# Folding the attention weights two banks a tick, and the first layer norm ahead of the folded weights

## The chip, the cores and the metric

One core of a Trainium2 chip runs the whole program. The metric is the device time of one execution, in microseconds (us). Engines are named as in the profile: PE is TensorE (matmuls), PEld its weight loads, DVE is VectorE, ACT is ScalarE, POOL is GpSimd, and SP is the engine whose queue issues nearly all DMAs here.

## What is computed

The input x has 4 images of 384 channels and 32 x 32 pixels, all in float32. Layer 0 adds a four-way selective scan of the group-normalised image, followed by a layer norm and a GELU. Layer 1 takes the pixels as tokens and adds causal attention and then a mixture of four expert networks, of which each token uses two. Cut to what matters:

```
x = x + gelu(layernorm(selective_scan_4_directions(groupnorm(x))))
t = tokens(x)                                  # 4 x 1024 x 384
n = layernorm(t)
q, k, v = n @ Wq, n @ Wk, n @ Wv
t = t + softmax(causal(q @ k.T * 384**-0.5)) @ v
t = t + top2_of_4_experts(layernorm(t))        # 384 -> 1536 -> 384 each
```

Since q k^T = n (Wq Wk^T) n^T, the kernel needs only the product of the two weights. And since the layer norm subtracts a mean that is linear in the token, the subtraction can be put into the weights: with the centring matrix C = I - 1/384, it uses C Wq Wk^T C and C Wv, and the tokens then only have to be scaled. Making these two 384 x 384 matrices is called folding here; it is done once.

## The kernel before

P = 128 partitions, M = 3 blocks of channels, B = 4 images, L = 1024 pixels.

**Ticks.** The program is written out by hand in ticks, by the loop at the end of `hybrid_kernel`. One tick handles one unit of the scan: 32 channels times 4 states of one image and direction, on 128 partitions and 1024 pixels. There are 4 x 192 units (`IMAGE` = 192). In each tick DVE multiplies (v, L561) and scans (h, L567), ACT makes the decay of two ticks ahead (da, L554), and POOL multiplies the scan of the tick before (L584). Every fourth tick PE sums four h into y with 16 matmul passes (L609). There are seven h buffers and three da buffers.

**What goes beside the scan.** Everything else is a Python generator that issues some instructions and then yields: "wait" with a number of ticks, "pe" with an estimate of PE time that is taken off a budget, or "inner", which puts the next piece into the following tick ahead of its scan. In a tick come, in this order: the decay, what was deferred to this tick, v and the product, inner pieces, the scan, y, the fetches for later ticks (`fetch`), one step of the image preparation (`preparation`, group norm and projections of an image to come), then the list `side` in its order, and last `waiting[0]`, which works off `behind(b)`: the attention and the experts of image b. Its budget per tick is `PACE_E` = 3.3 us of estimated PE time and, during the attention, `PACE_A` = 4.4.

**One image after another.** When the last unit of image b has been summed, `evict` starts `finish(b)`, layer 0's layer norm and GELU (side list), and appends `behind(b)`, which waits until `finish(b)` has put b into `finished`. By the code this takes from tick 195 to tick 206 for image 0 and from 387 to 398 for image 1. `behind(0)` is through in tick 397. After tick 768 there are no more scans, and what is left of image 3 runs alone.

**Shared buffers.** Four PSUM banks (two until tick 192) and eight SBUF slots are shared by all generators; `take` waits for a tick in which one is free, `give` returns it. Both lists are first in, first out. `project_dt` (L408 onwards) of the preparation needs four slots at once and two banks at a time; `layernorm`, as `finish` uses it, needs two banks for `mu` (L652), three slots for squares (L672), and a bank for `var` (L679); its remaining steps are a subtraction on DVE (L660), a square root on ACT (L687), a reciprocal (L692), the spread `rb` (L698) and a product (L708). `finish` then adds x (L893).

**The fold.** In tick 192 `second()` opens new pools: `a0` with one buffer and `ht` with two, of 12 KB a partition each. `fold` is started. It loads the three weights, makes the two centring blocks on DVE (L728), and then takes one bank a job: six `pwt` jobs (18 matmul passes each, L746), which turn and centre one third of Wq or Wk; three `pg` jobs (6 passes, L757) for the product; three `pwv` jobs (6 passes, L769) for the centred Wv. Each job waits a tick, is copied out by ACT (L751, L762, L774), and only then is the next begun. `g_d` and `wv_d` in HBM receive the result (L765, L777), and `folded` is set; by the code, in tick 208. `w_extra` in `a0` holds Wv and the centring blocks.

**The first attention.** `attention(b)` waits for `folded`, takes four slots and loads the folded weights (L962, L964), scales the tokens in `scaled_tokens` (squares L905, `var_at` L914, `rs_at` L923, L925, L927 and L929, `rb_at` L934, and `axn` L948), and goes on to `pq` (L980), `pv` (L991) and the scores (L1009).

Of the kernel before, what the change touches and what calls it, by code (L numbers as in the profile page):

```python
# [8 lines left out]
F32 = mybir.dt.float32  # L9
AF = mybir.ActivationFunctionType  # L10
ALU = mybir.AluOpType
# [4 lines left out]
P = 128  # L16
B = 4
C = 384
M = C // P
HW = 32  # L20
L = HW * HW
# [28 lines left out]
def hybrid_kernel(  # L50
# [22 lines left out]
    nc = tc.nc  # L73
# [44 lines left out]
    class Shared:  # L118
# [20 lines left out]
        def give(self, *names):  # L139
# [33 lines left out]
    g_d = dram.tile([P, M, C], F32, tag="g", name="g_d")  # L173
    wv_d = dram.tile([P, M, C], F32, tag="wv", name="wv_d")
# [75 lines left out]
    scale = float(C) ** -0.5  # L250
# [463 lines left out]
    folded = []  # L714

    def fold():

        extra = pools["a0"].tile([P, M, L], F32, tag="a0", name="w_extra")
        extra = extra.rearrange("p m l -> p (m l)")
        vs = extra[:, : 2 * M * C].rearrange("p (j c d) -> p j c d", j=2, c=M)
        centre = extra[:, 2 * M * C : 2 * M * C + 2 * P].rearrange("p (j d) -> p j d", j=2)
        nc.sync.dma_start(vs[:, 0], wv.rearrange("(c p) d -> p c d", p=P))
        for same in range(2):
            nc.vector.scalar_tensor_tensor(  # L728
                centre[:, same, :], ident, float(same), mean_w, ALU.mult, ALU.subtract
            )  # L730
        def square(name):
            t = pools["ht"].tile([P, M, L], F32, tag="ht", name=name)
            t = t.rearrange("p m l -> p (m l)")[:, : 2 * M * C]
            return t.rearrange("p (j c d) -> p j c d", j=2, c=M)

        raw = square("w_raw")
        for j, w in enumerate((wq, wk)):
            nc.sync.dma_start(raw[:, j], w.rearrange("(c p) d -> p c d", p=P))
        wt = square("w_t")
        yield "wait", 2  # L740
        for j in range(2):
            for d in range(M):
                ps = yield from banks.take(f"pwt_{j}_{d}")
                for c in range(M):
                    for o in range(M):
                        nc.tensor.matmul(  # L746
                            ps[:, c * P : (c + 1) * P], raw[:, j, o, d * P : (d + 1) * P],
                            centre[:, int(o == c), :], start=(o == 0), stop=(o == M - 1),
                        )
                yield "wait", 1  # L750
                nc.scalar.copy(wt[:, j, d, :], ps[:, :C])  # L751
                banks.give(f"pwt_{j}_{d}")
        g = square("g_s")[:, 0]
        for m in range(M):
            ps = yield from banks.take(f"pg_{m}")
            for d in range(M):
                nc.tensor.matmul(  # L757
                    ps[:, :C], wt[:, 0, d, m * P : (m + 1) * P], wt[:, 1, d, :],
                    start=(d == 0), stop=(d == M - 1),
                )  # L760
            yield "wait", 1
            nc.scalar.activation(g[:, m, :], ps[:, :C], AF.Copy, scale=-scale)  # L762
            banks.give(f"pg_{m}")
        yield "wait", 1
        nc.sync.dma_start(g_d, g)  # L765
        for m in range(M):
            ps = yield from banks.take(f"pwv_{m}")
            for c in range(M):
                nc.tensor.matmul(  # L769
                    ps[:, :C], centre[:, int(c == m), :], vs[:, 0, c, :],  # L770
                    start=(c == 0), stop=(c == M - 1),
                )
            yield "wait", 1
            nc.scalar.copy(vs[:, 1, m, :], ps[:, :C])  # L774
            banks.give(f"pwv_{m}")
        yield "wait", 1
        nc.sync.dma_start(wv_d, vs[:, 1])  # L777
        folded.append(1)


# [119 lines left out]
    def scaled_tokens(b, yb):  # L900

        sqs = []
        for c in range(M):
            sq = yield from slots.take(f"sq_at_{b}_{c}", P, L)
            nc.scalar.activation(sq, yb[:, c, :], AF.Square)  # L905
            sqs.append(sq)

        var = yield from banks.take(f"var_at_{b}")
        for o, src in ((NH * P, [yb[:, c, :] for c in range(M)]), (0, sqs)):
            for h in range(NH):  # L910
                for c in range(M):
                    for q in range(4):
                        k = h * 512 + q * P
                        nc.tensor.matmul(  # L914
                            var[32 * q : 32 * (q + 1), o + h * P : o + (h + 1) * P],
                            mean_w[:, :32], src[c][:, k : k + P],
                            start=(c == 0), stop=(c == M - 1), tile_position=(0, 32 * q),
                        )
                yield "pe", 1.0
        slots.give(*[f"sq_at_{b}_{c}" for c in range(M)])  # L920
        rs = one.tile([P, NH, P], F32, tag=f"rs{NH}", name=f"rs_at_{b}")
        flat = rs.rearrange("p h t -> p (h t)")
        nc.scalar.activation(flat, var[:, NH * P : 2 * NH * P], AF.Square)  # L923
        yield "inner", 0
        nc.vector.tensor_tensor(flat, var[:, : NH * P], flat, ALU.subtract)  # L925
        banks.give(f"var_at_{b}")
        nc.scalar.activation(rs, rs, AF.Sqrt, bias=eps)  # L927
        yield "wait", 1
        nc.vector.reciprocal(rs, rs)  # L929
        backs = []  # L930
        for h in range(NH):
            rb = yield from banks.take(f"rb_at_{b}_{h}")
            for q in range(4):
                nc.tensor.matmul(  # L934
                    rb[:, q * P : (q + 1) * P],
                    ident[:, 32 * q : 32 * q + 1].to_broadcast([P, P]), rs[:, h, :],
                    start=True, stop=True,
                )
            backs.append(rb)
            yield "pe", 1.0  # L940
        while b > 0 and b - 1 not in stored:

            yield "wait", 1
        xn = pools["a0"].tile([P, M, L], F32, tag="a0", name=f"axn_{b}")
        yield "inner", 0
        for h in range(NH):
            s = bass.ts(h, 512)
            nc.vector.tensor_tensor(  # L948
                xn[:, :, s], yb[:, :, s], backs[h].unsqueeze(1).to_broadcast([P, M, 512]), ALU.mult
            )  # L950
            banks.give(f"rb_at_{b}_{h}")
        return xn

    def attention(b, yb, fx0):

        alone = b == B - 1
        while not folded:
            yield "wait", 1
        gw_ = []
        for name, w in ((f"wg_{b}", g_d), (f"wv_{b}", wv_d)):  # L960
            ta = yield from slots.take(f"{name}a", P, 2, C)
# [1 line left out]
            tb = yield from slots.take(f"{name}b", P, C)  # L963
            nc.sync.dma_start(tb, w[:, 2, :])  # L964
            gw_.append((ta[:, 0, :], ta[:, 1, :], tb))
        xn = yield from scaled_tokens(b, yb)
        qt = pools["ht"].tile([P, M, L], F32, tag="ht", name=f"qt_{b}")
        vt = pools["ht"].tile([P, L // P, C], F32, tag="ht", name=f"vt_{b}")

# [4 lines left out]
        for h in range(NH):  # L974
            for m in range(M):
                s = bass.ts(h, 512)
                name = f"pq_{b}_{m}_{h}"
                ps = yield from banks.take(name)
                for c in range(M):
                    nc.tensor.matmul(  # L980
                        ps, gw_[0][c][:, m * P : (m + 1) * P], xn[:, c, s],
                        start=(c == 0), stop=(c == M - 1),
# [4 lines left out]
        for i in range(L // P):  # L987
            name = f"pv_{b}_{i}"
            ps = yield from banks.take(name)
            for c in range(M):  # L990
                nc.tensor.matmul(  # L991
                    ps[:, :C], xn[:, c, i * P : (i + 1) * P], gw_[1][c],
                    start=(c == 0), stop=(c == M - 1),
# [411 lines left out]
    while t < NU + 4 or waiting or side or due or inner or parked:  # L1405
# [5 lines left out]
        if t == IMAGE:  # L1411
            second()
            side.append(fold())
# [77 lines left out]
```

## Time and profile before

| | us |
|---|---|
| three executions | 3745.99, 3749.89, 3752.34 |
| median | 3749.89 |
| the profiled execution, own time | 3747.14 |
| its span in the profile | 3745.0 |
| span until the end of image 0's scans (tick 192) | 675.3 |
| first matmul `pq` of attention 0, 1, 2, 3 | 767.3, 1580.6, 2392.6, 3143.9 |
| TensorE and VectorE busy in the last 663 us | 641.0, 87.9 |

The span runs from the first to the last instruction of the profile; 2.1 us of the execution lie outside it. All times in the text that follows are microseconds from the start of the span. A line of a timeline gives start, duration, engine, source line, operation, output and inputs with buffer numbers left out, and the count of instructions merged in it; brackets give the idle time of the engine before it and who ended it. Matmuls in float32 appear as two passes each, so a job of nine matmuls shows as 18.

### The profile page before, as it was taken

The page shows a single profiled execution, that of the slowest core. Times are in us where ns is not written, and L with a number is a line of the kernel's source. Part 1 is how long each engine was busy: PE and PEld are TensorE (multiplying, and loading weights), DVE is VectorE, ACT ScalarE, POOL GpSimd, SP SyncE. Part 2 cuts the span into 40 slices and gives each one's busy share as a digit, 9 for nine tenths or more (in the row PEclk, how much of TensorE's full clock was granted, in tenths as well). Part 3 has the DMA queues.
Part 4 walks back from the last instruction along what each step waited for, and adds up shares of the span by engine and source line. Part 5 has one row for each costly group of instructions (what it writes and reads, how often), then busy time and mean ns, then how long its engine had stood idle before and what let it go on. Part 6 is the DMA issues. An engine that isn't in the chain of part 4 may idle for free. (4 is left out here: it accounts for less than half of the span.)

```text
span 3745.0 us, 35189 instructions
## 1 busy us (share of the span) xinstructions
PE 3350.6 (89%) x11891; PEld 1529.0 (41%) x11891; DVE 2961.6 (79%) x2084; ACT 2085.8 (56%) x2832; POOL 1817.8 (49%) x776
## 2 busy tenths in 40 slices
PE   4666667789999999898999999889999998999999
PEld 1333333345333343344333344454344444544444
DVE  5999899988998998989998999999999982210000
ACT  4788888556666555566655555455554552412121
POOL 2777777555565565545555665455665650000000
PEclk7677777899999999999999999899999999999999
DMA  6665666645665756436666665455657551322321
GB/s 204 219 233 199 208 218 221 215 145 199 235 222 201 260 206 230 155 138 228 217 221 229 201 210 192 146 182 188 223 192 240 179 182 38 92 82 83 96 82 53
DMA packets 408019, 680.03 MB, mean 182 GB/s; under 512 B 33520, under 2 KB 279968, under 8 KB 407840
## 3 DMA queue, kind: packets, MB, share of 16 engines
q1 hardware_dynamic: 401632, 677.40, 53.0%
q8 instruction: 94, 1.54, 0.2%
q10 hardware_dynamic: 6208, 0.39, 0.1%
q14 instruction: 85, 0.70, 0.1%
HBM read 605.16 MB, written 72.55 MB: 181 GB/s over the span
## 5 line engine op out<-in xcount | busy, mean ns | idle before, releaser
L584 POOL TENSOR_TENSOR h<-h,bc 128x1024 f32<-128x1024 f32 x768 | 1816.7, 2370 | 1264.9 <-DVE v L561 1058.3
L567 DVE TENSOR_TENSOR_SCAN h<-da,v 128x1024 f32<-128x1024 f32 x768 | 1748.4, 2283 | 48.4 <-PE v L872 17.3
L554 ACT ACTIVATE da<-dt,a 128x1024 f32<-128x1024 f32 x768 | 886.5, 1162 | 868.1 <-DVE h L567 759.3
L1297 PE MATMUL fy<-ht,w 128*128 128x512 f32 x2304 | 1019.8, 599 | 7.5 <-ACT ht L1261 5.9
L1272 PE MATMUL ph<-fx,w 128*128 128x512 f32 x2304 | 1019.1, 598 | 3.8 <-DMA w<-in_w 2.9
L561 DVE TENSOR_TENSOR v<-du,bc 128x1024 f32<-128x1024 f32 x664 | 842.8, 1269 | 61.9 <-DMA du<-dts 25.9
L1297 PEld LDWEIGHTS fy<-ht,w 128*128 128x128 f32 x2304 | 435.6, 191 | 580.3 <-issue 551.0
L1272 PEld LDWEIGHTS ph<-fx,w 128*128 128x128 f32 x2304 | 433.4, 191 | 579.6 <-issue 529.5
L609 PE MATMUL y<-h,sel 128*32 128x512 f32 x3072 | 493.3, 657 | 91.2 <-POOL h L584 89.2
L1257 ACT ACTIVATE ht<-ph,b1s 128x512 f32<-128x512 f32 x384 | 257.9, 679 | 471.0 <-PE ph L1272 469.2
L1306 DVE SCALAR_TENSOR_TENSOR fy<-fy,b2s,tw 128x512 f32<-128x512 f32 x96 | 72.0, 750 | 423.0 <-PE fy L1297 423.0
L609 PEld LDWEIGHTS y<-h,sel 128*32 128x32 f32 x3072 | 96.6, 115 | 399.3 <-issue 220.3
L850 ACT ACTIVATE st<-turn,bt 128x128 f32<-128x128 f32 x832 | 244.2, 554 | 0.0
L872 PE MATMUL v<-ident,st 128*128 128x128 f32 x832 | 147.5, 337 | 86.2 <-DVE h L567 85.4
L1261 ACT ACTIVATE ht<-ht 128x3072 f32<-128x3072 f32 x64 | 176.9, 2764 | 0.8
L872 PEld LDWEIGHTS v<-ident,st 128*128 128x128 f32 x832 | 121.7, 175 | 127.7 <-DVE h L567 74.2
L554 ACT ACT_TABLE_LOAD x99 | 127.0, 1283 | 18.7 <-DMA dt<-dts 12.3
L425 PE MATMUL pdt<-xd,wdt 12*128 12x512 f32 x184 | 88.0, 813 | 45.7 <-ACT dt L433 22.6
L1079 PE MATMUL po<-pt,vt 128*128 128x256 f32 x480 | 102.8, 364 | 7.1 <-ACT pt L971 7.1
L1009 PE MATMUL ss<-axn,qt 128*128 128x512 f32 (+3 forms) x288 | 102.3, 503 | 3.9 <-ACT yb L1096 3.9
L1079 PEld LDWEIGHTS po<-pt,vt 128*128 128x128 f32 x480 | 90.4, 192 | 22.3 <-ACT pt L971 10.1
L1009 PEld LDWEIGHTS ss<-axn,qt 128*128 128x128 f32 x288 | 51.5, 196 | 47.1 <-issue 33.5
(208 smaller groups left out, 1612.3 us busy)
## 6 DMA issues: line engine op xcount, KB each, us to landing
bc<-rows SPq DMA_DIRECT2D x384, 512.0 KB, 4.7
w<-in_w SPq DMA_DIRECT2D x384, 384.0 KB, 6.0
dt<-dts SPq DMA_DIRECT2D x192, 512.0 KB, 4.5
du<-dts SPq DMA_DIRECT2D x192, 512.0 KB, 6.6
dts<-dt SPq DMA_DIRECT2D x48, 512.0 KB, 4.7
dts<-du SPq DMA_DIRECT2D x48, 512.0 KB, 5.3
fx<-t2d SPq DMA_DIRECT2D x12, 768.0 KB, 5.5
tw<-mkd SPq DMA_DIRECT2D x32, 256.0 KB, 6.2
```

The lines of the kernel that those rows point to most:

```text
L554: u["decay"] = nc.scalar.activation(u["da"], spread["dt4", n], AF.Exp, scale=a4[:, g, u["q"] : u["q"] + 1])
L561: return nc.vector.tensor_tensor(u["v"], spread["du4", n], spread["bc", n][:, 0, :], ALU.mult)
L567: nc.vector.tensor_tensor_scan(u["h"][:, ::step], u["da"][:, ::step], u["v"][:, ::step], 0.0, op0=ALU.mult, op1=ALU.add,)
L584: product = units[n]["product"] = nc.gpsimd.tensor_tensor(h, h, spread["bc", n][:, 1, :], ALU.mult)
L609: units[n]["row"] = nc.tensor.matmul(y, sel, h, start=first, stop=last, tile_position=(0, jj * DJ))
L850: nc.scalar.activation(st[:, 4 * h + t, :].rearrange("p (d i) -> p i d", i=NI)[:, i, :], ps[h][:, t * P : (t + 1) * P], AF.Copy, scale=bt[ ...
L872: nc.tensor.transpose(u["v"][:, t * P : (t + 1) * P], st[:, t, u["j"] * P : (u["j"] + 1) * P], ident)
L1079: nc.tensor.matmul(pv[:, o:], vt[:, j, m * P : (m + 1) * P], pts[step][j // 4][:, j % 4, o:], start=(alone and j == 0), stop=(j == nj - 1),)
L1257: nc.scalar.activation(ht[:, f, :], ps, AF.Identity, bias=bias)
L1261: nc.scalar.activation(ht, ht, AF.Gelu)
L1272: nc.tensor.matmul(ps, tiles[n][:, c, (f % 2) * P : (f % 2 + 1) * P], xns[h][:, c, :], start=(c == 0), stop=(c == M - 1),)
L1297: nc.tensor.matmul(pss[m], tiles[n][:, f, :], hts[fh][:, f, :], start=(fh == 0 and f == 0), stop=(fh == 1 and f == FH - 1),)
```

## The change

`fold` no longer uses `a0`. Wv and the centring blocks go into three of the shared slots (`va`, `vb`, `centre`), Wq and Wk are loaded first, and the result is collected in one `ht` tile, `both`. The jobs are functions that issue their matmuls into a bank and return the copy that is to follow. `by_twos` takes two banks at once, issues two jobs, and makes the two copies in the next tick, in which it also begins the next two jobs. The product and the centring of Wv form one list of six jobs. The slots are given back before the stores. `attention(0)` makes `scaled_tokens` first, then waits for `folded`, and then loads the folded weights; the attentions of the other images keep their order, without the wait.

```diff
-        extra = pools["a0"].tile([P, M, L], F32, tag="a0", name="w_extra")
...
         raw = square("w_raw")
         for j, w in enumerate((wq, wk)):
             nc.sync.dma_start(raw[:, j], w.rearrange("(c p) d -> p c d", p=P))
+        va = yield from slots.take("va", P, 2, C)
+        vb = yield from slots.take("vb", P, C)
+        centre = yield from slots.take("centre", P, 2, P)
+        wvs = wv.rearrange("(c p) d -> p c d", p=P)
+        nc.sync.dma_start(va, wvs[:, :2, :])
+        nc.sync.dma_start(vb, wvs[:, 2, :])
...
+        def by_twos(what, jobs):
+            for n in range(0, len(jobs), 2):
+                some = jobs[n : n + 2]
+                while not banks.ready(len(some)):
+                    yield "wait", 1
+                names = [f"{what}_{n + i}" for i in range(len(some))]
+                moves = [f(banks.now(name)) for f, name in zip(some, names)]
+                yield "wait", 1
+                for move in moves:
+                    move()
+                banks.give(*names)
+
+        yield "wait", 2
+        pairs = [(j, d) for d in range(M) for j in range(2)]
+        yield from by_twos("pwt", [lambda ps, j=j, d=d: turned_weight(j, d, ps) for j, d in pairs])
+        both = square("g_s")
+        jobs = [lambda ps, m=m: product(m, ps) for m in range(M)]
+        yield from by_twos("pg", jobs + [lambda ps, m=m: centred(m, ps) for m in range(M)])
+        slots.give("va", "vb", "centre")
+        nc.sync.dma_start(g_d, both[:, 0])
+        nc.sync.dma_start(wv_d, both[:, 1])
+        yield "wait", 1
         folded.append(1)
...
     def attention(b, yb, fx0):
 
         alone = b == B - 1
-        while not folded:
-            yield "wait", 1
+        if b == 0:
+            xn = yield from scaled_tokens(b, yb)
+            while not folded:
+                yield "wait", 1
         gw_ = []
         for name, w in ((f"wg_{b}", g_d), (f"wv_{b}", wv_d)):
             ta = yield from slots.take(f"{name}a", P, 2, C)
...
-        xn = yield from scaled_tokens(b, yb)
+        if b > 0:
+            xn = yield from scaled_tokens(b, yb)
```

`turned_weight`, `product` and `centred` issue the same matmuls as before into the bank they are given, and return the same ScalarE copies.

More of the change, by code (lines that the diff above doesn't have):

```diff
@@ L716, in fold @@
     def fold():
-        extra = pools["a0"].tile([P, M, L], F32, tag="a0", name="w_extra")
[L723 to L730, printed above, removed]
         def square(name):
@@ L738, in fold, with turned_weight, product @@
             nc.sync.dma_start(raw[:, j], w.rearrange("(c p) d -> p c d", p=P))
-        wt = square("w_t")
[L740 to L749, printed above, removed]
-                yield "wait", 1
[L751 to L755, printed above, removed]
+        va = yield from slots.take("va", P, 2, C)
[4 more added lines that the diff above has]
+        nc.sync.dma_start(vb, wvs[:, 2, :])
+        vs = (va[:, 0, :], va[:, 1, :], vb)
+        for same in range(2):
+            nc.vector.scalar_tensor_tensor(
+                centre[:, same, :], ident, float(same), mean_w, ALU.mult, ALU.subtract
+            )
+        wt = square("w_t")
+        def turned_weight(j, d, ps):
+            for c in range(M):
+                for o in range(M):
+                    nc.tensor.matmul(
+                        ps[:, c * P : (c + 1) * P], raw[:, j, o, d * P : (d + 1) * P],
+                        centre[:, int(o == c), :], start=(o == 0), stop=(o == M - 1),
+                    )
+            return lambda: nc.scalar.copy(wt[:, j, d, :], ps[:, :C])
+        def product(m, ps):
             for d in range(M):
@@ L760, in fold, with centred @@
                 )
[L761 to L767, printed above, removed]
+            return lambda: nc.scalar.activation(both[:, 0, m, :], ps[:, :C], AF.Copy, scale=-scale)
+        def centred(m, ps):
             for c in range(M):
                 nc.tensor.matmul(
-                    ps[:, :C], centre[:, int(c == m), :], vs[:, 0, c, :],
+                    ps[:, :C], centre[:, int(c == m), :], vs[c],
                     start=(c == 0), stop=(c == M - 1),
                 )
-            yield "wait", 1
-            nc.scalar.copy(vs[:, 1, m, :], ps[:, :C])
-            banks.give(f"pwv_{m}")
+            return lambda: nc.scalar.copy(both[:, 1, m, :], ps[:, :C])
+        def by_twos(what, jobs):
[18 more added lines that the diff above has]
+        nc.sync.dma_start(wv_d, both[:, 1])
         yield "wait", 1
-        nc.sync.dma_start(wv_d, vs[:, 1])
         folded.append(1)
@@ L956, in attention @@
         alone = b == B - 1
-        while not folded:
-            yield "wait", 1
+        if b == 0:
+            xn = yield from scaled_tokens(b, yb)
+            while not folded:
+                yield "wait", 1
         gw_ = []
```

## The prediction, made before the changed kernel ran

> **What bounds the kernel now.** I read the page's first part, then busy time by stage around the changed code, then who waited for whom on VectorE there, and last the timelines of each engine between 670 and 790 us.
>
> ```profile
> PE 3350.6 (89%) x11891; PEld 1529.0 (41%) x11891; DVE 2961.6 (79%) x2084; ACT 2085.8 (56%) x2832; POOL 1817.8 (49%) x776
> ```
>
> TensorE and VectorE are both full, but at different times, so the shares of the span decide nothing. The stage table (us; busy time of each engine, granted clock, DMA share) cuts where the changed code stands:
>
> ```profile
> core 0: us, PE busy (x) PEld busy (x) DVE busy (x) ACT busy (x) POOL busy (x), PEclk, DMA share, GB/s
> 675.30:765.50 90.20, 65.41 (x409) 37.76 (x409) 84.60 (x54) 53.25 (x60) 45.60 (x20) 0.78 0.53 190
> 765.50:1520.00 754.50, 727.50 (x2440) 317.18 (x2440) 705.23 (x504) 464.75 (x499) 423.00 (x180) 0.99 0.61 211
> 1520.00:1580.60 60.60, 43.84 (x276) 19.64 (x274) 59.82 (x42) 32.53 (x33) 28.82 (x13) 0.86 0.52 184
> ```
>
> From 675 to 765 us, where the weights are folded and the first attention waits, VectorE is busy 84.6 of 90.2 us and sets the pace; TensorE idles 25 us at a clock of 0.78. From 765 to 1520 us the first image's attention and experts hold TensorE for 727.5 of 754.5 us. From 1520 to 1580 us that work has run out: TensorE idles 17 of 60.6 us, VectorE is full. So work of image 0 that starts earlier finds a valley both in front of it and behind it.
>
> ```profile
> DVE rs_l L692 <- ACT rs_l L687: 1.8, 1, 1.8
> DVE rs_at L925 <- ACT rs_at L923: 1.6, 1, 1.6
> DVE axn L948 <- PE rb_at L934: 1.0, 1, 1.0
> ```
>
> These are all the named waits of VectorE from 676 to 772 us: 4.4 us in three places (columns: us in total, times, longest). That is the most which any reordering there can win on the engine that bounds.
>
> The ticks: each tick holds one scan of VectorE (L567). The two centre operations of `fold` come right behind the scan of tick 192, so scans can be numbered from there.
>
> ```profile
> 677.50 0.52 DVE L728 SCALAR_TENSOR_TENSOR w_extra<-ident,mean_w 128x128 f32<-128x128 f32 x2
> ...
> 740.41 1.43 DVE L893 TENSOR_TENSOR yb<-xr,yb 128x1024 f32<-128x1024 f32 x1
> ...
> 765.48 3.46 DVE L948 TENSOR_TENSOR axn<-yb,rb_at 128x1536 f32<-128x1536 f32 x2 [1.02 <-PE rb_at L934]
> ```
>
> Counted so, the last addition of `finish(0)` (740.41) stands ahead of scan 206, and `axn` (765.48) ahead of scan 211. `finished` is thus set in tick 206, and attention 0 held back until `folded`, in tick 208. TensorE and the DMA queue say the same:
>
> ```profile
> 711.43 4.21 PE L746 MATMUL pwt<-w_extra,w_raw 128*128 128x128 f32 x18
> 715.57 1.10 PE L679 MATMUL var_l<-sq_l,mean_w 128*32 128x128 f32 x24
> ...
> 739.38 0.64 PE L914 MATMUL var_at<-yb,mean_w 128*32 128x128 f32 x16
> ...
> 751.15 0.66 PE L914 MATMUL var_at<-sq_at,mean_w 128*32 128x128 f32 x8 [8.17 <-ACT sq_at L905]
> ...
> 767.29 1.98 PE L980 MATMUL pq<-axn,wg_0a 128*128 128x512 f32 x4
> ```
>
> ```profile
> 747.23 0.54 SPq L777 DMA_DIRECT2D wv_d<-w_extra  x1
> 747.82 0.42 SPq L962 DMA_DIRECT2D wg_0a<-g_d  x1
> ...
> 752.44 0.32 SPq L962 DMA_DIRECT2D wv_0a<-wv_d  x1
> 752.81 0.44 SPq L964 DMA_DIRECT2D wv_0b<-wv_d  x1
> 753.34 22.78 SPq L533 DMA_DIRECT2D bc<-rows  x4
> ```
>
> The loads of the folded weights issue at 747.8 to 753 us, 15 us before the first `pq` needs them: hidden today.
>
> **What the skill says.** *PSUM — Partial Sum Buffer*, "PSUM: the matmul accumulator": 8 banks of 2 KiB a partition. Here y and v take two each, so four are shared; two a tick is half of them. No run here shows the size itself. *ScalarE: Activation LUTs*, "What ACT_TABLE_LOAD costs": about 1283 ns, plus a drain of about 1380 ns. The trace has 1283 ns as the mean of 99, but no drain (a load from 716.17 for 1.28 us, the square root at 717.47), so I take 1.28 us. *TensorE: Matmul & The Clock Gate*, "What's actually happening": the clock halves after an idle window of some 3.4 us and comes back after as much steady work. The trace agrees in kind: granted clock 0.78 in the thin stage, 0.99 in the full one, and a `pwt` job of 18 matmuls at 2.17 to 2.3 us, once 4.21. *Perfetto Trace Analysis*, "Per-engine timelines" (DMA, HWDGE): the window shown for a queue's DMA leaves out the moving of data. The trace agrees: `wg_0a` shows 0.42 us on the queue and 5.6 us to landing.
>
> **The change, part by part.**
>
> *1. The fold itself.* Same matmuls (6 `pwt`, 3 `pg`, 3 `pwv` jobs), same 12 copies, same two centre operations. By the code: pairs of `pwt` in ticks 194, 195, 196; `pg` 0 and 1 in 197; `pg` 2 with `pwv` 0 in 198; `pwv` 1 and 2 in 199; stores in 200; `folded` in 201 instead of 208. Banks suffice: with two held by the fold, `finish(0)` still gets `mu` in 195 and 196 and `var` in 198.
>
> *2. Its crowd on TensorE.* In ticks 194 to 199 TensorE now has 6 x 2.3 (`pwt`) + 6 x 2.1 (`pg`, `pwv`) + 2 x 2.7 (`mu`) + 2.2 (one row) + 2 x 0.9 (`var`) = 36 us. From 681.3 us, in order and at that speed, the first half of `mu` ends at 693, the second at 700.5, the second `var` at 717.2; before it ended at 716.7. The second half of the subtraction L660 would start at 700.1 and waits 0.4 us. The reciprocal L692 starts at about 718.2 against 717.97, although a multiplication of 1.43 us (L441) has left its front (part 3). VectorE so loses 0.2 + 1.43 = +1.7 us. Bounds: 0, if the matmuls run as the fastest do; +12, if the clock is low (rival B).
>
> *3. Three slots for va, vb and centre.* From 192 to 200 three of eight slots are gone. `finish(0)` takes three more in 198, so two are left, and `project_dt` of image 1 (last m, second pair), which wants four in tick 198, starts in 201. All it issues moves along: one ScalarE copy (1.97 us), four softplus pieces with their table loads, four `pdt` matmuls, two multiplications of VectorE (1.43 and 1.37), four stores on SP's queue. Its results are first needed near tick 347: nothing waits. SP's stores then stand behind the `xr` loads of tick 204, which helps those. The square root of L687 no longer follows a softplus; I count one more table load, 1.28 us on ScalarE, covered by its lead of two ticks (it is busy 53 of 90 us). The moved multiplications cost VectorE the same later. Uncovered it would be +1.3.
> `preparation(1)` also ends three ticks later, so all of `preparation(2)` to about tick 348 shifts by three; due from 379 on.
>
> *4. The layer norm beside the fold.* `folded` no longer gates; `finished` in 206 does. But in 206 the budget is still at the slower pace, 3.3, not 4.4: the four steps of 1.0 use it up, and the rest of `scaled_tokens` goes on in 207. The subtraction L925 falls in 208 (before: 209), `axn` in 210 (before: 211). So two ticks of waiting win one. ScalarE's squares and square now have a tick between them and L925: its wait of 1.64 us goes. What is late next is `rb_at` at `axn`, 1.0 us, as before.
>
> *5. Weights after the layer norm.* The four loads (1.15 MB) are now issued in tick 210, behind the `bc` loads of tick 209. SP is held there by the product of tick 208, in today's trace until 753.3 us. Shifted by the 0 to 2 us of the parts above, `wg` issues at about 754.5 and lands 5.6 us later, at 760 to 761, as its measured time says; half of `axn` would be done at about 762. Cost between 0 (landed in time) and +4 us (if the `bc` megabyte in front delays it by its own landing time, 4.7, less what slack there is). I take +1. Behind a waiting `pq` stand the row matmuls of y, which free h buffers (seven), two ticks of cover. Pools: `axn` no longer waits for `w_extra` to be stored, nothing today.
>
> *6. What an earlier tick is worth.* TensorE gets `pq` one tick, 3.5 us (1.23 for v + 2.29 for the scan), earlier. The work of image 0 then ends one tick sooner, in tick 396, not 397 by the code, while attention 1 starts when image 1's own `finish` is through, in tick 398, whatever image 0 does. So the tick won in front (-3.5) is a tick of plain scan more behind (+3.5): 0. Images 1 to 3 and the tail after the last scan (663 us from 3082) start on ticks fixed by the scans.
>
> Sum: -3.5 + 3.5 + 1.7 - 1.6 + 1.0 = +1 us. To that comes the shift of `preparation(2)` against the experts (part 3). VectorE's multiplications L441 waited 13 us for TensorE and ScalarE between 765 and 1520 us; where a projection falls behind a long group of `fy` is luck, and I give it 0 with 5 us either way. The profiled execution took 3747.1 us (span 3745.0), 2.8 below the median of the three times shown. +1 on the median is 3751; between the two I take 3750.
>
> **The rivals.**
> *A, faster:* the earlier start is not given back. If work of image 0 also spills over its end, two ticks (7 us) plus the lost wait (1.6) come off the median: 3741. For it: PE is 96% busy from 765 to 1520. Against: the 17 us of idle TensorE behind it, and attention 1's start, which doesn't depend on it. Chance 0.12.
> *B, slower:* the crowd of part 2 at a low clock. If the 36 us run at 0.78, as this stage does on average, they take 46, and VectorE's reciprocal, with everything behind it in order, waits 10 us longer: 3760. It decides once the second `var` ends later than some 722 us, and nothing afterwards gives it back, as VectorE bounds there. For it: the one `pwt` job of 4.21 us. Against: steady work should raise the clock. Chance 0.11.
> *C, slower:* the shifted `preparation(2)` meets the long groups more often and L441's 13 us double, with TensorE idling for part of it: +8, 3758. For it: the same waits are 17.5 us one image later. Against: a wait of VectorE for a full TensorE costs little. Chance 0.10.
> *D, the change doesn't do what it says:* if banks or slots made `finish(0)` late by a tick, attention 0 would start as it does now: +2 at most, inside the forecast.
>
> **How the numbers follow.** A measurement of this kernel tells about 0.2%, 7.5 us, from no change. Forecast (no change, 3743 to 3757) 0.67; A 0.12; B 0.11; C 0.10. Faster 0.12, same 0.67, slower 0.21. The range 3741 to 3760 holds the forecast's own and reaches to where A and B stand, leaving out their outer halves.
>
> **What would show it.** Right: `wv_d` stored near 715 us; `var_at` straight behind the additions of `finish(0)`; no wait at L925; `axn` one scan earlier, counted from the centre operations; `pq` waiting for `wg_0a` for a few us at most; TensorE's valley before attention 1 a tick wider. Wrong: the second `var` of `finish(0)` past 722 us, a `pq` that waits over 4 us, or attention 1 starting on another tick than 398.

## The result, and the profile after

| | before | changed |
|---|---|---|
| median of 13 executions each, us | 3750.81 | 3760.06 |
| lowest and highest, us | 3745.99, 3754.15 | 3755.33, 3765.23 |
| ratio of the times, 95% interval | | 1.0025 (1.0017 to 1.0034) |
| the profiled execution, us | 3747.14 | 3765.23 |
| its span, us | 3745.0 | 3763.1 |

The change costs 9.3 us, 6 to 13 by the interval. The two profiles lie 18.1 us apart, because the one of before is 3.7 us faster than its median and the one of the changed kernel 5.2 us slower than its own; stages are therefore compared below, and sizes taken from medians.

The page of the changed kernel has the work of before; its first line and one group of matmuls are enough to see what is new (line, engine, operation, output and inputs, count, busy us, mean ns, idle time before them and who ended most of it):

```profile
PE 3367.0 (89%) x11891; PEld 1534.2 (41%) x11891; DVE 2963.5 (79%) x2084; ACT 2087.2 (55%) x2833; POOL 1817.6 (48%) x776
...
L1287 PE MATMUL ph<-fx,w 128*128 128x512 f32 x2304 | 1030.3, 603 | 15.9 <-DMA w<-in_w 8.7
```

The same group in the kernel before:

```profile
L1272 PE MATMUL ph<-fx,w 128*128 128x512 f32 x2304 | 1019.1, 598 | 3.8 <-DMA w<-in_w 2.9
```

Counts are equal, except for one more on ScalarE, the table load counted in part 3. But the first expert product, `ph`, now idles 15.9 us in front of its matmuls, 8.7 of them for weights; before it was 3.8 and 2.9.

**Where the time went.** Each tick has one scan, so the two executions can be laid over each other tick by tick. Starts of the scan, us, read from the trace:

```
tick                        192    211    240    244    248    256    396    767
before                    675.3  768.9  890.4  911.9  934.3  965.6 1550.7 3078.5
changed                   676.0  767.4  891.5  921.0  943.2  990.4 1563.8 3093.0
changed, after tick 192           -2.2   +0.4   +8.4   +8.2  +24.1  +12.4  +13.8
```

At tick 240, with all of the fold, of the layer norm and of attention 0 done, the two stand 0.4 us apart. Between ticks 240 and 256 the changed kernel loses 24 us, and gets half of it back by tick 396. From there to the last scan they differ by 1.4, and behind it by another 3.6 us, within what the profiles of all kernels below show there (666.5 to 670.1 us, in no relation to the edits). The stages as the profile has them, first of before, then of the changed kernel, cut at the ticks 192, 240, 256 and 396:

```profile
675.30:890.40 215.10, 181.01 (x930) 106.18 (x930) 202.11 (x154) 129.52 (x178) 113.28 (x48) 0.90 0.46 167
890.40:965.60 75.20, 75.19 (x291) 35.19 (x289) 65.96 (x53) 55.26 (x59) 37.83 (x16) 0.98 0.72 247
965.60:1550.70 585.10, 565.96 (x1771) 226.40 (x1775) 552.08 (x371) 347.78 (x338) 332.71 (x141) 0.99 0.64 217
```

```profile
676.00:891.50 215.50, 184.13 (x964) 109.05 (x964) 202.37 (x154) 131.38 (x179) 113.24 (x48) 0.88 0.46 165
891.50:990.40 98.90, 86.85 (x273) 36.30 (x273) 68.48 (x71) 55.62 (x61) 37.66 (x16) 0.88 0.61 209
990.40:1563.80 573.40, 557.70 (x1754) 222.70 (x1756) 550.39 (x354) 347.32 (x337) 332.72 (x141) 0.99 0.64 217
```

(Columns: stage, its length, busy time of PE, PEld, DVE, ACT and POOL with counts, granted clock, DMA share, GB/s.) In the 16 ticks of the second row TensorE was busy without a gap; now it idles 12 of 98.9 us, and its clock falls from 0.98 to 0.88. That is the hand-over from attention 0 to its experts. It lies some 180 us behind the fold, in code that the diff doesn't touch. Of the 12 us, 6.9 are one wait, shown next; 3.2 more come at 948 us, where a later `ph` waits for ScalarE.

The 24 us are not all one loss. By the ticks above, 8 of them arise between 240 and 244, around that one wait, and 16 between 248 and 256. Of these some 12 come back by tick 396, and at least in part they are work that has only moved forward: from tick 240 to 256 TensorE now makes 38 passes of `fy`, against 24 before.

**What stands there.** TensorE in the kernel before, then in the changed one (start, us, operation; in brackets idle time and its releaser):

```profile
896.42 2.74 PE L1123 MATMUL pgate<-gw,fx 128*128 128x4 f32 x24
899.02 2.82 PE L392 MATMUL pxd<-x,wx 128*128 128x512 f32 x6
...
903.62 2.84 PE L392 MATMUL pxd<-x,wx 128*128 128x512 f32 x6
906.30 7.89 PE L1272 MATMUL ph<-fx,w 128*128 128x512 f32 x18
```

```profile
889.02 2.74 PE L1138 MATMUL pgate<-gw,fx 128*128 128x4 f32 x24
898.62 5.49 PE L1287 MATMUL ph<-fx,w 128*128 128x512 f32 x6 [6.86 <-DMA w<-in_w]
903.90 3.06 PE L392 MATMUL pxd<-x,wx 128*128 128x512 f32 x6
```

The loads of the first expert weights, before and changed:

```profile
895.37 2.76 SPq L1216 DMA_DIRECT2D w<-in_w  x4
890.13 4.17 SPq L1231 DMA_DIRECT2D w<-in_w  x4
```

Before, projections of image 2 (`pxd`) stand between the gate and the first `ph`, which starts at 906.3, while the weights had been issued at 895.4. In the changed kernel the projections come later, `ph` stands right behind the gate, and its weights were issued at 890.1. TensorE waits 6.9 us for them, and its first job behind the wait takes 5.49 us, where six passes of the same kind take 2.74 further on. The load itself was slow: `ph` starts 8.5 us behind its issue, while the page's median for these loads is 5.8 us from issue to landing. ScalarE and VectorE stop with it. First ScalarE, then VectorE, both of the changed kernel:

```profile
891.36 0.84 ACT L1111 COPY yb<-po 128x512 f32<-128x512 f32 x2
904.14 0.69 ACT L1272 ACTIVATE ht<-ph,b1s 128x512 f32<-128x512 f32 x1 [11.95 <-PE ph L1287]
904.73 0.20 ACT L1158 ACTIVATE sc<-sc 128x16 f32<-128x16 f32 x1
```

```profile
895.50 2.29 DVE L567 TENSOR_TENSOR_SCAN h<-da,v 128x1024 f32<-128x1024 f32 x1
904.97 0.17 DVE L1160 TENSOR_REDUCE red<-sc 128x4 f32<-128x16 f32 x1 [7.18 <-ACT sc L1158]
```

In ScalarE's program the exponential of the gate (0.2 us) stands behind the move of `ph` out of its bank. ScalarE idles 12 us ahead of that move, and the exponential, whose input VectorE finished at 894.3, starts only behind it, at 904.7. In VectorE's program the gate's sum waits for the exponential, and behind it stands the next scan, which has nothing to do with either. One load that nothing hides so becomes 7.2 us of idle time on VectorE, whose scans make the ticks.

**Why the load is bare.** By the code's own ticks, the fold's three slots keep `project_dt` of image 1 waiting from tick 198 to 201; its end moves with it, and the start of `preparation(2)` on the engines (its image is loaded three ticks before) from 219 to 222. In tick 240 of before, `pxd` holds the last free bank just when the experts of image 0 want one, so `ph` stands one tick behind the issue of its weights (240 and 241), with two `pxd` jobs ahead of it. In the changed kernel the first `pxd` is not due before 240; in tick 239 a bank is free, and the experts issue the load and the first `ph` in the same tick.

### The profile page after: what moved, and what is told of

Read it like the earlier page. It is cut to its first block, busy times and chain, and to the rows that moved or that the text cites. A ratio compares the mean times of both kernels' runs of the same rounds, so it can differ in the third digit from the quotient of the medians.

```text
span 3763.1 us, 35200 instructions
## 1 busy us (share of the span) xinstructions
PE 3367.0 (89%) x11891; PEld 1534.2 (41%) x11891; DVE 2963.5 (79%) x2084; ACT 2087.2 (55%) x2833; POOL 1817.6 (48%) x776
## 5 line engine op out<-in xcount | busy, mean ns | idle before, releaser
L1287 PE MATMUL ph<-fx,w 128*128 128x512 f32 x2304 | 1030.3, 603 | 15.9 <-DMA w<-in_w 8.7
L609 PE MATMUL y<-h,sel 128*32 128x512 f32 x3072 | 500.9, 662 | 96.0 <-POOL h L584 94.0
```

The costliest lines, as they stand in the source:

```text
L609: units[n]["row"] = nc.tensor.matmul(y, sel, h, start=first, stop=last, tile_position=(0, jj * DJ))
L1287: nc.tensor.matmul(ps, tiles[n][:, c, (f % 2) * P : (f % 2 + 1) * P], xns[h][:, c, :], start=(c == 0), stop=(c == M - 1),)
```

## The experiments

Most change one thing in one of the two kernels; four put two edits together, as said there. "Rest" is the pause that the preparation makes after a projection, 12 ticks; only the one behind image 1's last projection is varied. Ratios are against the kernel before on the same chip; its median was 3750.3 to 3751.4 us in the three groups. Each version ran 5 to 21 times.

### First group: which of the shifts costs

The preparation of image 2 back in its old tick, in the changed kernel:

```diff
-                yield "wait", 0 if b == 0 and m == 0 else 12
+                last = b == 1 and m == M - 1 and pair == 1
+                yield "wait", 0 if b == 0 and m == 0 else 9 if last else 12
```

> The changed kernel, but the rest after image 1's last projection is 9 ticks, not 12, so that the preparation of image 2 starts in tick 219 as in the kernel before; all else, the first ph in the tick of its weights' load included, stays. Theory 1 (the shifted preparation of image 2 costs the time): back to about 3751 us, and the scan of tick 256 within 4 us of the kernel before. Theory 2 (the first expert matmul stands in the same tick 239 as the issue of its weights, and TensorE waits for them): 3758 us or more, and TensorE waits 5 to 8 us for w at the first ph. Rival 3 (attention 0 and its experts one tick earlier, whatever the rest): about 3760 us.

Measured: 3747.11 us, ratio 0.9988 (0.9982 to 0.9995). No wait for w, although `ph` and load still share tick 239: two `pxd` jobs now stand ahead of the gate, so TensorE is that much behind its program and comes to `ph` at 901.1 us, 10.9 us after the load's issue at 890.2. In the changed kernel it had come there, and begun to wait, after 1.6 us (gate done at 891.8, issue at 890.1). Theory 1 said 3751 and came near with the time, though its other sign failed: from tick 192 to 256 this version takes 299.2 us, 8.9 more than the kernel before, and is ahead only by tick 396. Rival 3 is out: the early attention alone costs nothing. That the wait would stay, as theory 2 said for this kernel, was wrong: the shared tick is harmful only where TensorE has no backlog ahead of it.

The same shift alone, in the kernel before (`15` in place of `9` in the lines above):

> The kernel before, but the rest after image 1's last projection is 15 ticks, so that the preparation of image 2 starts three ticks later, in 222, as in the changed kernel; the first ph stays a tick behind its weights' load (240 and 241). Theory 1: about 3760 us. Theory 2: about 3751 us, with a wait for w at the first ph of under 4 us. Rival 3: 3751 us.

Measured: 3742.60 us, ratio 0.9972 (0.9963 to 0.9982). All theories missed: a preparation three ticks late, by itself, makes the kernel 9 us faster. Lateness as such is not the cost. In this kernel `ph` stays a tick behind its load and doesn't wait.

The load uncovered as in the changed kernel, but with a pause behind it:

```diff
                 while not slots.ready():
                     yield "wait", 1
                 weights()
+                if b == 0 and n == 0:
+                    yield "wait", 2
```

> The changed kernel, but the experts of image 0 wait two ticks between the issue of their first weights (tick 239) and the first ph (241); the preparation of image 2 stays three ticks late. Theory 2: TensorE's wait for w at the first ph goes, and the time falls by 6 to 9 us, to 3751 to 3754. Theory 1: 3758 to 3761 us, since the shifted preparation stays. Rival 3: between the two, about 3756.

Measured: 3740.99 us, ratio 0.9966 (0.9954 to 0.9979), lowest of all and below both kernels. The wait for w is gone. The gain of 19 us against the changed kernel is over twice the wait, so the pause did something else as well: it also starts the experts of image 0 two ticks later against the preparation, and all but the first of their four weight loads with them. Which of these brings the rest was not tested.

The new order of attention 0 alone, in the kernel before:

```diff
-        while not folded:
-            yield "wait", 1
+        if b == 0:
+            xn = yield from scaled_tokens(b, yb)
+            while not folded:
+                yield "wait", 1
...
-        xn = yield from scaled_tokens(b, yb)
+        if b > 0:
+            xn = yield from scaled_tokens(b, yb)
```

> The kernel before with one part of the change alone: attention 0 scales its tokens before it waits for the fold, and loads the folded weights afterwards; the fold itself stays one bank a job and without shared slots. Attention 0 is then as early as in the changed kernel (first pq in tick 210), the preparation of image 2 starts in 219 as before, and the first ph stands in the tick of its weights' load, 239. Theory 1: about 3750 us. Theory 2 or rival 3: 3757 to 3760 us; under theory 2 TensorE waits 5 to 8 us for w at the first ph.

Measured: 3746.56 us, ratio 0.9989 (0.9981 to 0.9997), no wait for w. This part of the change is a small gain, not a cost. The preparation, the load and the first `ph` stand in the same ticks here as in the first experiment (219, 239, 239), with the old fold in place of the new one, and the time is the same within 1 us: the new fold by itself costs nothing that shows.

### Second group: the wait by itself, and the parts of the change

The wait alone, every other instruction left in its tick, slot and bank:

```diff
+            if b == 0 and n == NB + 2:
+                t = yield from slots.take("w_0_0", P, M, 2 * P)
+                nc.sync.dma_start(t, w1[0, :, : 2 * P].rearrange("(c p) f -> p c f", p=P))
+                first_w.append(t)
             if n >= 3 and n % 2 == 0:
                 yield from values((n - 3) // 2)
...
+        if first_w:
+            tiles[0] = first_w.pop()
+            fetched[0] = 1
         load(0)
```

> The changed kernel with one load moved: the first expert weights of image 0 are loaded in tick 236 and not in 239, into the same slot; every other instruction keeps its tick, its slot and its bank (first ph in 239, preparation of image 2 from 222). This takes TensorE's wait for w away and nothing else. Theory 2 in its narrow form (the wait of 6.9 us, the slower matmuls behind it and what stands behind them in ScalarE's order): 3748 to 3752 us. Theory 2 in its wide form (the wait sets off all that the changed kernel loses against the version with a pause of two ticks): about 3741 us. If the pause helped only by moving the experts against the preparation: 3757 to 3760 us.

Measured: 3753.75 us, ratio 1.0011 (1.0004 to 1.0017). TensorE at the same place:

```profile
891.76 2.74 PE L1142 MATMUL pgate<-gw,fx 128*128 128x4 f32 x24
894.36 2.82 PE L1294 MATMUL ph<-fx,w 128*128 128x512 f32 x6
```

`ph` follows the gate without a gap, in 2.82 us, and the median falls by 3760.06 - 3753.75 = 6.3 us (5.8 when each is taken against the kernel before of its own group; the two intervals leave about 4 us either way). So the bare load is worth some two thirds of the loss. The trace has the repair where the wait was: from tick 240 to 244 this version takes 20.8 us, the changed kernel 29.5, the kernel before 21.5. From 248 to 256 it takes 48.4 us, against 47.2 and 31.3: the longer time of those ticks doesn't come from the wait. The expectation's narrow form was somewhat too generous (3748 to 3752), the wide form wrong: 3 us above the kernel before, and 13 above the version with the pause, remain.

Both edits together (rest 9 and pause of two):

> The changed kernel with both edits: the pause of two ticks before the first ph (241) and the preparation of image 2 back in tick 219. If the loss comes from the two together (late preparation leaves nothing ahead of the first ph to cover its load), taking both away brings no more than either: 3743 to 3749 us. If each has a cost of its own that adds up (13 and 19 us on the medians so far): below 3735 us.

Measured: 3744.22 us, ratio 0.9981 (0.9974 to 0.9988). They don't add up: late preparation and shared tick do harm together, and taking away either is enough.

The changed kernel with its fold kept out of the shared slots:

```diff
-        va = yield from slots.take("va", P, 2, C)
-        vb = yield from slots.take("vb", P, C)
-        centre = yield from slots.take("centre", P, 2, P)
...
+        extra = pools["a0"].tile([P, M, L], F32, tag="a0", name="w_extra")
+        extra = extra.rearrange("p m l -> p (m l)")
+        va = extra[:, : M * C].rearrange("p (c d) -> p c d", c=M)
+        centre = extra[:, M * C : M * C + 2 * P].rearrange("p (j d) -> p j d", j=2)
...
-        slots.give("va", "vb", "centre")
```

> The changed kernel without its use of shared slots: Wv and the centring blocks stay in the a0 buffer, two banks a tick and the new order of attention 0 stay. By the code image 1's last projection then stands in tick 198 again, finish(0) is two ticks later for want of banks (208), first pq in 212, preparation of image 2 from 219, first ph a tick behind its load (241 and 242). Theory (slots, the late preparation and the uncovered load are one chain): no wait for w, 3745 to 3752 us. If two banks a tick cost by themselves: 3756 us or more.

Measured: 3746.77 us, ratio 0.9991 (0.9984 to 0.9997), no wait for w at the first `ph`. Two banks a tick cost nothing that shows, and without the slots the loss is gone, although attention 0 here starts later than in both kernels (212). As the preparation, the load and `ph` all move here, this tests the chain as a whole and not one link of it.

The changed kernel with attention 0 in the old order:

```diff
-        if b == 0:
-            xn = yield from scaled_tokens(b, yb)
-            while not folded:
-                yield "wait", 1
+        while not folded:
+            yield "wait", 1
...
-        if b > 0:
-            xn = yield from scaled_tokens(b, yb)
+        xn = yield from scaled_tokens(b, yb)
```

> The changed kernel with the old order in attention 0: wait for the fold, load the folded weights, then scale the tokens. By the code first pq in 210, preparation of image 2 from 222, first ph in the tick of its load, 239, all as in the changed kernel. Theory (slots, late preparation, uncovered load): 3757 to 3762 us, with 5 to 8 us of TensorE waiting for w. If loading the folded weights behind the layer norm is what costs: 3751 us.

Measured: 3762.31 us, ratio 1.0033 (1.0020 to 1.0045), with a wait of 6.98 us for w at the first `ph`. The order has no part in the loss.

### Third group: the loss without the change, and what is left

The kernel before with a rest of 18 (as in the second experiment) and no part of the change:

> The kernel before, with no part of the change, but a rest of 18 ticks after image 1's last projection: the preparation of image 2 from 225. By the code nothing of it then takes a bank ahead of the first ph, which falls into the tick of its weights' load, 240. Theory (the loss is the late preparation that uncovers the load, and no part of the fold): TensorE waits 5 to 8 us for w at the first ph, and the time is 9 to 15 us above that of the same kernel with 15 ticks, 3752 to 3758 us. If the changed fold were needed for it: about 3743 us.

Measured: 3760.75 us, ratio 1.0021 (1.0013 to 1.0030). This is the loss of the change, with the same line on TensorE:

```profile
893.47 2.74 PE L1124 MATMUL pgate<-gw,fx 128*128 128x4 f32 x24
904.48 5.06 PE L1273 MATMUL ph<-fx,w 128*128 128x512 f32 x6 [8.27 <-DMA w<-in_w]
```

With a rest of 15 this kernel is 9 us faster than with 12, with 18 it is 9 us slower; with 18, no `pxd` stands ahead of the gate or behind it, and TensorE has caught up when `ph` comes. The step from 15 to 18 was expected at 9 to 15 us and is 18; how much of it is the wait was not taken apart in this kernel.

What is left when the wait is gone. In ticks 246 to 249 of the version with the early load, ScalarE makes a square root, a GELU and two softplus pieces; and between ticks 240 and 256 VectorE's longest waits are these (us in total, times, longest):

```profile
DVE du L441 <- PE fy L1319: 5.9, 1, 5.9
DVE fx L708 <- PE rb_ff L698: 5.7, 1, 5.7
DVE v L561 <- PE y L609: 4.2, 1, 4.2
```

So the GELU was moved, on top of the early load:

```diff
-                defer(2, lambda ht=ht: gelu(ht))
+                first = b == 0 and h == 0 and e == 0 and fh == 0
+                defer(5 if first else 2, lambda ht=ht: gelu(ht))
```

> The changed kernel with its first expert weights loaded in tick 236 (no wait for w) and one thing more: the first GELU of the experts of image 0 goes to ScalarE three ticks later (249 and not 246), still ahead of its first use in 250. It tests what is left of the loss once the wait is gone. Theory (a pile on ScalarE: in ticks 246 to 249 the square root of the second layer norm, this GELU and the two softplus pieces of the late preparation, each with table loads, so that TensorE waits 3.2 us for a bank and VectorE 5.7 for rb): 3747 to 3751 us, the wait of TensorE for ht gone. If ScalarE's order there has no part: 3752 to 3756 us.

Measured: 3751.80 us, ratio 1.0002 (0.9994 to 1.0010): 2 us below the version with the early load alone, with intervals that overlap. TensorE's wait of 3.2 us for `ht` ahead of a `ph` is gone (2.1 us ahead of `fy` stand in its place), and VectorE's for `rb` fell from 5.7 to 1.1, but a multiplication of the late preparation now waits longer:

```profile
DVE du L441 <- PE fy L1320: 7.9, 1, 7.9
```

The pile on ScalarE is there, but taking it apart seems to move the wait more than it removes it: inconclusive.

The early load, and the preparation another three ticks later (rest 15):

> The changed kernel with its first expert weights loaded in tick 236, and the preparation of image 2 another three ticks later, from 225 (its first pdt in 250, not 247). Theory (a late preparation costs where its softplus pieces meet the second layer norm and the GELU, not as such): 3743 to 3750 us. If the later the worse: 3757 us or more.

Measured: 3752.80 us, ratio 1.0005 (0.9999 to 1.0012). Neither form: moving the softplus pieces away from the GELU brings nothing to speak of.

The pause, and rest 15:

> The changed kernel with the pause of two ticks before the first ph, and the preparation of image 2 from 225, three ticks later than there. It is the search for a version that beats both: the pause gave 3741 us with 222 and 3744 with 219. Theory: no wait for w, and 3738 to 3747 us.

Measured: 3749.33 us, ratio 0.9997 (0.9989 to 1.0005). No wait for w, but above the range that was expected, and 8 us above the pause with the preparation from 222, which stays the lowest of all.

### All of them side by side

Tick in which `preparation(2)` starts on the engines; ticks of the first weights' load and of the first `ph`; wait of TensorE for w there; stages between ticks in the profiled execution; median. All us but the ticks.

```
                              prep 2  load  ph   wait   240-256  192-396  median
before                          219   240  241    -       75.2    875.4  3750.8
changed                         222   239  239   6.9      98.8    887.8  3760.1
changed, old order              222   239  239   7.0      98.8    886.7  3762.3
before, rest 18                 225   240  240   8.3      95.2    884.3  3760.8
changed, load early             222   236  239    -       90.8    880.5  3753.8
  and GELU late                 222   236  239    -       86.4    877.3  3751.8
  and rest 15                   225   236  239    -       85.5    879.5  3752.8
changed, pause of two           222   239  241    -       81.1    862.6  3741.0
  and rest 15                   225   239  241    -       84.2    874.9  3749.3
  and rest 9                    219   239  241    -       80.6    870.3  3744.2
changed, rest 9                 219   239  239    -       84.5    871.9  3747.1
before, norm first              219   239  239    -       83.5    870.8  3746.6
changed, fold in a0             219   241  242    -       77.9    872.0  3746.8
before, rest 15                 222   240  241    -       83.5    865.8  3742.6
```

The stages are of one execution and the medians of all, so they are not to be subtracted to the microsecond. But in all 14 rows the median less the stage from tick 192 to 396 is 2872 to 2878 us, and the profiled execution's own time less that stage 2871 to 2881, in no order with the medians: no effect of the edits shows in the rest of the kernel. The three rows with a wait for w are the three slowest, at 3760 us and above; no other is above 3754.

## Why the prediction was wrong

It forecast no change, 3750 us; measured are 3760, just beyond the range's upper end.

Right, step by step: parts 1 to 5 worked out the stage from tick 192 to the first `pq` and met it. All ticks came as worked out from the code (`folded` in 201, `finished` in 206, `axn` in 210). VectorE's waits there, in the changed kernel:

```profile
DVE yb L905 <- ACT yb L900: 1.3, 1, 1.3
DVE rs_l L692 <- ACT rs_l L687: 1.2, 1, 1.2
```

The wait at the subtraction in `scaled_tokens` is gone, as said; so is the one of 1.0 us at `axn`, which was to stay. In its place 1.3 us stand at an addition of `finish(0)`, not foreseen. TensorE's crowd, and the stores and loads of the folded weights:

```profile
714.35 0.86 PE L679 MATMUL var_l<-sq_l,mean_w 128*32 128x128 f32 x24
...
762.28 1.98 PE L995 MATMUL pq<-axn,wg_0a 128*128 128x512 f32 x4 [0.95 <-DVE axn L960]
```

```profile
714.96 0.33 SPq L788 DMA_DIRECT2D wv_d<-g_s  x1
...
755.26 0.54 SPq L976 DMA_DIRECT2D wg_0a<-g_d  x1
```

The second `var` ends at 715.2 (forecast 717.2; rival B needed 722), `wv_d` is stored at 715.0 (near 715), `wg_0a` issues at 755.3 (754.5), and `pq` waits 0.95 us for `axn` and nothing for the weights (forecast 1, up to 4). The crowd, priced at +1.7 us of VectorE, cost nothing: the reciprocal started at 716.8, not 718.2. (One reading was short: rival B's evidence, one `pwt` job of 4.21 us, has a second beside it in the trace of before, of 3.69 us at 701.9.) Against the forecast of about +0.1 in this stage, tick 211 shows -2.2 us. Part 6 holds too: image 0's work ends in tick 396, attention 1 starts in 398, and from tick 396 to 767 the two kernels differ by 1.4 us.

Wrong: one sentence of part 3, "`preparation(1)` also ends three ticks later, so all of `preparation(2)` to about tick 348 shifts by three; due from 379 on", and the term made of it in the sum, "luck", 0 with 5 us either way. The shift was seen, and asked only when its results are due. What it covers was not asked: in the kernel before, its `pxd` jobs take the bank and the time in front of the first `ph`, and so hide the load of the first expert weights. The tick that attention 0 gains, which parts 4 and 6 had right and priced at nothing, is needed for the harm as well: with the preparation three ticks late but attention 0 where it was (rest 15 in the kernel before), a `pxd` still takes the last bank in tick 240, `ph` comes in 241, and nothing waits. A tick earlier, `ph` comes in 239, ahead of every `pxd`. The sum priced the two shifts one by one; what lies between the two pieces of work changes with both.

With the cover gone the load costs about 6 us (6.3 on the medians), which the version with the early load measured with every other instruction in its tick, slot and bank. The other 3 of the 9.3 us are that version's distance to the kernel before. They go when the preparation is put back (3747), and also when the experts start two ticks later (3741), so they hang on how the two stand to each other; which of their collisions make them was not settled.

Rival C had the right source, the shifted preparation, and the wrong place. It named VectorE's multiplications L441 as waiting twice as long behind `fy`; from the first `pq` to tick 390 they waited 4.5 + 2.5 = 7.0 us for ScalarE and TensorE in the changed kernel (and 4.7 for a DMA), against 13.3 before. Rival B's time was met to the microsecond by chance: its crowd behind the fold cost nothing, and the loss arises elsewhere and in another way. Rival A is out: the tick won was given back, as forecast.

Still open: why the eleven rows without a wait spread over 13 us, from 3741 to 3754. The kernel before is itself one of the slower of them, at rest 12; with rest 15 it is 9 us faster. The shift of the preparation alone moved that kernel by -9 us (rest 15) and +9 us (rest 18, with the wait), so "5 us either way" was also too narrow.

## What to carry to other kernels

When a step is delayed, ask not only who needs its results, but what its instructions were covering: instructions queued ahead and banks that are taken can hide a transfer by accident, and the cover can be some 180 us away from the edit. Issue the first weights of a stage some ticks ahead of their first use by design; here that is one early load, and the wait was gone in all three versions that have it, though they still took 0.4 to 3.5 us more than the kernel before. And in a program whose side work is placed by counters, a shift of three ticks can be worth as much as the edit that caused it, in either sign (9 us less and then 18 us more here, for two such steps), so a change should be judged with the shift undone as well.

## What was not expected of the hardware

One wait of TensorE for a load of 384 KB went through three engines in order: 6.9 us on TensorE, 12.0 on ScalarE, 7.2 on VectorE, where the instruction that waited was a sum over 128 x 16 values. Behind the wait the first job of six matmul passes took 5.49 us, and 5.06 in the other kernel that waited, against 2.74 to 2.84 where there was no gap. *TensorE: Matmul & The Clock Gate*, "What's actually happening", describes such a clock, halved after an idle window and restored by steady work. The traces agree: behind idle times of 6.9 and 8.3 us the granted clock was 0.50 and 0.55 while these jobs ran, and 0.96 and 1.00 in the 6 and 10 us that followed.
